# Attention and mixture of experts on one core: tokens sorted into lists per expert in DRAM for seven of eight groups

## The chip, the core and the metric

The kernel runs on one core of a Trainium2 chip. The core has five engines that work side by side, each with its own queue of instructions, which it executes in order: TensorE (PE) multiplies matrices, VectorE (DVE) and ScalarE (ACT) work element by element, GpSimd (POOL) does the same and issues some DMAs, and SyncE (SP) issues most of the others. Engines wait for one another through semaphores. SBUF is the on-chip memory of 128 partitions; PSUM holds matmul results. The metric is the device time of one execution in microseconds (us); the median of three runs counts. Less is better.

## The reference

The program is one transformer layer with the norms after the additions, on `x` of 2 sequences of 2048 tokens with 512 features, in float32. Attention has 16 query heads of 32 features that share one key and one value head, and is causal. The second half is a mixture of 8 experts, of which each token takes two.

```python
qkv = einsum('bsd,ed->bse', x, Wqkv_w) + Wqkv_b            # q: 512, k: 32, v: 32
scores = einsum('bqhd,bkd->bhqk', q, k) / sqrt(32)         # causal mask, softmax
ctx = einsum('bhqk,bkd->bqhd', softmax(scores), v)
x = layernorm(x + ctx @ out_w.T + out_b)
expert_scores = x @ router_w.T                             # 8 scores a token
top_scores, selected = top_k(expert_scores, 2)             # softmax of the two
h = silu(x_bf16[e's tokens] @ w1[e]) * (x_bf16[e's tokens] @ w3[e])    # 512 -> 128
routed = h @ w2[e]                                         # 128 -> 512
x = layernorm(x + sum over the two experts of top_scores * routed)
```

In the reference only the two chosen experts compute a token (`ragged_dot` over tokens sorted by expert).

## The kernel before

The 4096 tokens are 32 tiles T of 128 (16 for each sequence); four tiles are a group G. One function, `run`, holds all. It is called once with `full=False`, and a second time under `tc.If(flag)` only if a flag that the first pass computes says that its numbers cannot be trusted (softmax without an exact row maximum overflowed); in the runs here it isn't taken.

Work is written as Python generators that `yield step(engine, us, ...)` before they issue instructions. At build time the class `Order` (L67) simulates the engines with these assumed durations, with latencies between engines (`LAT`), buffers (`rings` of named tokens, and four PSUM `banks`), priorities and due times (`Due`), and so fixes one order of instructions for each of PE, ACT, DVE and POOL. The wrapper `InOrder` (L239) issues them, which is why nearly every line of the profile is L248. DMAs on SP are not held to that order: the framework's scheduler places them. On the chip each engine then follows its fixed list; where an assumed duration was wrong, the engine waits.

Per group, `project` (L519) loads four tiles `xg`, transposes them on PE, and computes keys, values and queries. Per tile, `attention` (L1067) goes through the tile's own key block and all earlier ones of the sequence, so that tile T has T modulo 16, plus one, **key steps**: 272 in all. A key step is: eight K=32 row-tiled score matmuls on PE into the PSUM tile `three` and one bank; two exponentials on ACT (`exponentials`, out to `acc` for the own block, to `pT` for the others); the product with the values on PE (`weigh`, tile `cs`); and an addition of `pT` into `acc` on DVE (`add_up`), which gives the row sums. The own block is masked by an `affine_select` on POOL before PE may use it. `pT` has three buffers. `three` has one, so PE writes the next scores only after ACT has read it.

At a tile's end `after` (L753) sums `acc` over keys on PE, forms the reciprocals on DVE, multiplies by the output weights on PE (`woT`), adds the residual `xr` (loaded by SP, bias added on POOL), and normalises (`layernorm`, L726: statistics on DVE, two tiny `r` operations on POOL, scaling on ACT).

`experts` (L841) then computes **all eight experts for every token** and multiplies by gates that are zero for six of them. For a tile: transposes and router (`route`, `gates`), 64 bf16 matmuls of 128x512 against w1 and w3 (`up`, `half`), tanh on ACT, a product with `a` on DVE, the gate on POOL (`a<-a,gt`), the product `h` on DVE, a DMA transpose `hT` on SP, 32 matmuls against w2 (`down`), the addition to `x` and a second layernorm. Groups 0 to 6 do this group by group, with due times some 16 tiles later, so that it fills gaps; the last group does it tile by tile. `x1` keeps up to four groups of 128x4x512 in SBUF until then. For the last tile, `last_sums` (L1187) adds the last two key blocks on PE instead of DVE; `judge` computes the flag's input before the last experts.

```python
def issue(self, ins):
    InOrder.last = ins
    return self.tc.keep_in_program_order(ins)
...
for c in range(NG):                                  # mm4: four column groups of 32
    mm(out[quad(c)], lhsT[:, quad(c)], rhs, **k)
```

Of the kernel before, what the change touches and what calls it, by code (L numbers as in the profile page):

```python
# [9 lines left out]
F32 = mybir.dt.float32  # L10
# [18 lines left out]
X1B = 4  # L29
# [37 lines left out]
class Order:  # L67
# [4 lines left out]
    LAT = {PE: 0.3, ACT: 0.15, DVE: 0.15, POOL: 0.15, SP: 0.0}  # L72
    LOOK = {DVE: 1.0}
    TURN = {FULL: 0.1, ROW: 0.2, COL: 0.115, TILE: 0.115}
    CAP = 5.0

    def __init__(self, banks, **rings):
        self.rings = {name: [n, []] for name, n in rings.items()}
        self.banks = [None] * banks
        self.busy = {e: 0.0 for e in self.LAT}  # L80
        self.sig = {}
        self.parked = []
        self.now = self.end = 0.0
        self.event = 0
        self.array = None
        self.count = 0
        self.dues = []
        self.held = {}
# [24 lines left out]
    def hold(self, ring, n):  # L113
        self.held[ring] = [self.take(ring) for _ in range(n)]
# [6 lines left out]
    def take_all(self, rings, t):  # L121
        slots = self.slots(rings.count(BANK), t)
        tokens = []
        for ring in rings:
            if ring == BANK:
                token = Token(ring)
                token.slot = slots.pop(0)
                token.before = self.banks[token.slot]
                self.banks[token.slot] = token
            else:  # L130
                token = self.take(ring)
            tokens.append(token)
        return tokens

    def slots(self, n, t):

        free = [i for i, k in enumerate(self.banks) if k is None or k.at is not None and k.at <= t + 1e-6]
        free.sort(key=lambda i: self.banks[i].at if self.banks[i] else 0.0)
        return free[:n]

    def room(self, rings):

        at = 0.0
        n = rings.count(BANK)
        if n:
            free = sorted(0.0 if k is None else k.at for k in self.banks if k is None or k.at is not None)
            if len(free) < n:
                return None
            at = free[n - 1]
        for i, ring in enumerate(rings):  # L150
            if ring == BANK:
                continue
# [30 lines left out]
    def run(self):  # L183
        while self.parked:
# [23 lines left out]
            if eng in self.LOOK and best[1][0].us > 1.0 and self.prio(best[1][0], urgent) > -0.9:  # L208

                for x in able:  # L210
                    s = x[1][0]
                    if (
                        s.eng == eng and self.prio(s, urgent) <= -0.9 and x[0] < t0 + self.LOOK[eng]
                        and x[0] <= best[0] + self.LOOK[eng]
                    ):
                        best = x
                        break
# [38 lines left out]
def mqa_postln_moe_postln(  # L256
# [22 lines left out]
    EB = 4  # L279
    scale = 1.0 / math.sqrt(HD)  # L280
# [15 lines left out]
    def mm4(out, lhsT, rhs, **k):  # L296
        for c in range(NG):
            mm(out[quad(c)], lhsT[:, quad(c)], rhs, **k)

    def tr4(out, in_):  # L300
        for c in range(NG):
            tr(out[quad(c), :], in_[:, quad(c)], ident)
# [14 lines left out]
    )  # L317
    warm = const.tile([P, 1], F32, name="warm")
# [4 lines left out]

    worst = const.tile([P, 1], F32, name="worst")
# [13 lines left out]

    def run(full):
# [5 lines left out]
        n_x1 = X1B - full  # L345
        x1p = es.enter_context(tc.tile_pool(name="x1p", bufs=n_x1))
        att = es.enter_context(tc.tile_pool(name="att", bufs=1))
        ptp = es.enter_context(tc.tile_pool(name="pt", bufs=3))
# [5 lines left out]
        if full:  # L354
# [19 lines left out]

        order = Order(
            NB, three=1, pT=3, acc=2, cs=1, c_sb=2, lT=1, ctxT=1, shT=3 if full else NSH, pmax=2, xg=1, xT=1,
            xr=2, qT=2, kv=GPB + 1, x1=n_x1, x1b=1, x1T=TG, a=2, h=2, hT=2,
# [46 lines left out]
        def load_weights():  # L424
            nat["wkv"] = ffn.tile([2 * HD, D], F32, tag="a", name="wkv_n")
            nat["wq"] = grp.tile([P, NHH, D], F32, tag="qT", name="wq_n", bufs=2)
            nat["wo"] = grp.tile([P, NHH, D], F32, tag="qT", name="wo_n", bufs=2)
            nat["wr"] = ffn.tile([E, D], F32, tag="a", name="wr_n")
            b_row = nat["b"] = ffn.tile([1, D + 2 * HD], F32, tag="x1T", name="b_row", bufs=TG)
# [7 lines left out]
        def turn_biases():  # L437
# [23 lines left out]
            free(order.held["x1T"][0])  # L461
# [45 lines left out]


        kT, v, qTs, kv_held, qT_held, st_x = {}, {}, {}, {}, {}, {}

        def load_x(G):
            b, gi = divmod(G, GPB)
            xg = grp.tile([P, TG, D], F32, tag="xg", name="xg")
            for t in range(TG):
                s0 = gi * GT + t * P
                nc.sync.dma_start(xg[:, t, :], x[b, s0 : s0 + P, :])
            return xg

        def project(G, due):  # L519
            hurry = -1.5 if G == 0 else None  # L520
            due = Due(due, 21.7)
            (hx,) = yield step(SP, 0.0, ["xg"])
            xg = load_x(G)
            st = {}

            def turn(t):
                (m,) = yield step(PE, 0.45, ["m"], array=FULL, lat=5.0 + 0.5 * t, prio=hurry, due=due)
                p_t = bank(m)
                for dc in range(NDC):
                    tr(p_t[:, dc * P : (dc + 1) * P], xg[:, t, dc * P : (dc + 1) * P], ident)  # L530
                if t == TG - 1:
                    free(hx)
# [214 lines left out]
        def add_keys(p_l, e, start, stop):  # L747
            for g in range(NG):
                mm(p_l[quad(g), :, :], ones, e[:, g, :, :], start=start, stop=stop)

        sums, contexts = {}, {}

        def after(T, acc, h):  # L753
# [3 lines left out]
            if T == seq[-1]:  # L757
                yield step(SP, 0.0, after=[("w", T, T % TPB - 2)])
            (h_xr,) = yield step(SP, 0.0, ["xr"])
            xr = grp.tile([P, D], F32, tag="xr", name="xr", bufs=2)  # L760
# [3 lines left out]
            if T == seq[-1]:  # L764
                yield step(SP, 0.0, after=[("l", T)])
            if T in sums:
                m, h_l, p_l = sums[T]
            else:
                m, h_l = yield step(PE, 0.87, ["m", "lT"], array=COL, due=due)
                p_l = bank(m, F32, (P, NHH, P))  # L770
                add_keys(p_l, acc, True, True)
# [4 lines left out]
            lT = att.tile([P, D // HD, HD], F32, tag="lT", name="lT")  # L776
# [8 lines left out]
            if T == seq[-1]:  # L785
                yield step(DVE, 0.7, after=[("c", T)])
            c_sb, h_c = contexts.pop(T)
            ctxT = att.tile([P, NHH, P], F32, tag="ctxT", name="ctxT")
# [5 lines left out]
            if T == seq[-1] and not full:  # L794
                spawn(judge())
# [12 lines left out]
            if t == 0:  # L808
                (x1_held[G],) = yield step(SP, 0.0, ["x1"])
                x1s[G] = x1p.tile([P, TG, D], F32, tag="x1", name="x1")  # L810
                mark("x1", G)
            yield step(DVE, 1.65, after=[("xr", T), ("x1", G)])
            y = x1s[G][:, t, :]
# [6 lines left out]
            if alone or t == TG - 1:  # L820
                spawn(
                    experts(G, [t] if alone else list(range(TG)), start_of((G + n_x1) * TG)),
# [3 lines left out]
        def judge():  # L826

            (h,) = yield step(DVE, 1.1, ["lT"])
            ok = att.tile([P, NT, D // HD], F32, tag="lT", name="ok")
            vec.tensor_scalar(ok, fine, LIMIT, None, ALU.is_le)  # L830
            vec.tensor_reduce(worst, ok, AX.XY, ALU.min)
            free(h)

        def residual(T, xr):
            yield step(POOL, 1.4, lat=3.0)
# [4 lines left out]

        def experts(G, ts, due):  # L841
            b, gi = divmod(G, GPB)
            x1 = x1s[G]
# [7 lines left out]
            x1b = ffn.tile([P, NDC, GT], BF16, tag="x1b", name="x1b", bufs=1)  # L851
# [3 lines left out]
            def route(t):  # L855
# [4 lines left out]
                for dc in range(NDC):  # L860
                    tr(p_t[:, dc * P : (dc + 1) * P], x1[:, t, dc * P : (dc + 1) * P], ident)
                yield step(ACT, 0.6)
                x1T = st["x1T", t] = ffn.tile([P, NDC, P], F32, tag="x1T", name="x1T", bufs=TG)
# [3 lines left out]
                if n > 1:  # L867
                    yield step(POOL, 1.05)
# [68 lines left out]
            def up(t, j):  # L937
# [8 lines left out]
                if j == 0:  # L946
                    st["h_h", t] = got[2]
                    st["h", t] = ffn.tile([P, E, FF], BF16, tag="h", name="h")
# [9 lines left out]
                a = ffn.tile([P, EB, FF], F32, tag="a", name="a")  # L958
# [6 lines left out]
                if n > 1:  # L965
                    yield step(POOL, 2.25)
# [33 lines left out]
            def down(t):  # L1000
# [4 lines left out]
                hT = ffn.tile([P, E, P], BF16, tag="hT", name="hT")  # L1005
# [21 lines left out]
                y = x1[:, t, :]  # L1027
# [3 lines left out]
                yield step(SP, 0.0)  # L1031
                s0 = gi * GT + t * P
                nc.sync.dma_start(out[b, s0 : s0 + P, :], y)
                if t == TG - 1:
                    free(x1_held[G])
# [31 lines left out]
        def attention():  # L1067
            for T in seq:
# [4 lines left out]
                for i, kt in enumerate([own] + list(range(own))):  # L1073
# [11 lines left out]
                    )  # L1085
                    qT = qTs[G]
# [26 lines left out]
        def exponentials(T, kt, parts, hp):  # L1113
# [18 lines left out]
            if kt == own:  # L1132

                yield step(POOL, 2.25, prio=-2.0)
# [10 lines left out]
        def weigh(T):  # L1145
# [5 lines left out]
            for i, kt in enumerate(kts):  # L1151
# [16 lines left out]
                if i == 0:  # L1168
                    spawn(add_up(T, [k for k in kts if k != own][: own - direct(T)]))
                    if direct(T):  # L1170
                        spawn(last_sums(T, kts[own + 1 - direct(T) :]))
                        spawn(after(T, None, None), True)
# [5 lines left out]
            c_sb = att.tile([P, D], F32, tag="c_sb", name="c_sb", bufs=2)  # L1178
            act.copy(c_sb, cs.rearrange("p h k -> p (h k)"))
            free(h_cs)  # L1180
            contexts[T] = c_sb, h_c
            mark("c", T)
            if not direct(T):
                yield step(SP, 0.0, after=[("sum", T)])
                spawn(after(T, *tiles.pop((T, own))))

        def last_sums(T, kts):  # L1187

            m, h_l = yield step(PE, 0.87, ["m", "lT"], array=COL, prio=-0.2, after=[("sum", T)])
            p_l = bank(m, F32, (P, NHH, P))  # L1190
            add_keys(p_l, tiles[T, T % TPB][0], True, False)
            for kt in kts:
                yield step(PE, 0.87, array=COL, prio=-0.2, after=[("p", T, kt)])
# [119 lines left out]
```

## Time and profile before

| what | value |
|---|---|
| runs | 1153.9, 1154.88, 1155.04 us; median 1154.88 |
| profiled execution | 1154.49 us, span on the core 1152.7 us |
| granted TensorE clock | 0.998 of full speed |
| attention's own key blocks start | T=0 at 40.5 us, T=10 at 271.9, T=16 (second sequence) at 562.9, T=26 at 812.6, T=31 at 1056.0 |
| last addition into `acc` ends | 1115.5 us |
| DMA | 40.94 MB, 36 GB/s over the span |
| two of PE's waits | PE `three` for ACT `pT` 21.4 us, PE `bank` for DVE `acc` 4.3 us |
| POOL's instructions `r` | shortest 543 ns, median 2487 ns (`r<-r,neg_half`, 128x1) |

The span runs from the first to the last instruction on the core; some 2 us of the execution's time lie around it. A group's mean is the time of one instruction from its start to its end; matmuls overlap one another, so the busy time of a group (the time in which at least one of them ran) is far less than count by mean. PE is busy for nearly the whole span, but it does four different things in turn, and the other engines' load rises with the number of key blocks of a tile: a late tile has fifteen additions on DVE, an early one none. So the span is best read in stages, cut where the tiles in the table start.

### The profile page before, as it was taken

How to read it: one execution, taken by the hardware profiler on the slowest of the kernel's cores; microseconds unless marked ns; L12 is line 12 of the kernel's file. 1: busy time of each engine (PE TensorE's matmuls, PEld its weight loads, DVE VectorE, ACT ScalarE, POOL GpSimd, SP SyncE). 2: the span in 40 equal slices, each digit the busy share in tenths (PEclk: the TensorE clock that was granted, in tenths of full speed). 3: DMA queues.
4: the chain of work that ended last, by engine and by line, in shares of the span. 5: the costliest groups of instructions: out<-in, count | busy, mean ns of one | idle time of the engine just before them, and what ended most of it. 6: DMA issues, size and time to landing. Idle time of an engine off the chain costs nothing.

```text
span 1152.7 us, 29615 instructions
## 1 busy us (share of the span) xinstructions
PE 1087.3 (94%) x13046; PEld 329.4 (29%) x13046; DVE 923.6 (80%) x1171; ACT 735.8 (64%) x839; POOL 452.2 (39%) x291
## 2 busy tenths in 40 slices
PE   8999999999999999999999999999999899899975
PEld 4322222222322233232222222223233233233222
DVE  2348767878998789989747877779989999999975
ACT  2455667576676677775656556666676667767561
POOL 3212432213451245445325324416556455345110
PEclk9999999999999999999999999999999999999999
DMA  9301001002110021111001000001011011011011
GB/s 253 75 17 56 10 10 48 11 11 56 30 47 1 11 66 29 38 30 38 19 20 56 20 10 19 20 20 38 20 37 40 20 26 42 19 30 48 20 29 31
DMA packets 57404, 40.94 MB, mean 36 GB/s; under 512 B 42729, under 2 KB 43753, under 8 KB 57266
## 3 DMA queue, kind: packets, MB, share of 16 engines
q1 hardware_dynamic: 47248, 34.63, 11.2%
q0 software_dynamic: 9360, 3.15, 2.4%
q8 instruction: 104, 1.70, 0.6%
q10 hardware_dynamic: 658, 1.18, 0.3%
q14 instruction: 34, 0.28, 0.1%
HBM read 25.58 MB, written 8.39 MB: 29 GB/s over the span
## 4 chain that ended last, share of the span: by engine, by line
PE 58%; DVE 28%; issue 5%; POOL 4%; ACT 4%; DMA 0%; DVEq 0%; ACTq 0%; POOLq 0%
PE bank L248 33%; DVE acc L248 15%; PE three L248 14%; PE cs L248 11%; ACT pT L248 2%; POOL r L248 2%; POOL a L248 2%; DVE st L248 2%; DVE x L248 2%; DVE h L248 2%; DVE lT L248 1%; DVE ctxT L248 1%; DVE a L248 1%; DVE fine L248 1%; DVE mx L248 1%
## 5 line engine op out<-in xcount | busy, mean ns | idle before, releaser
L248 DVE TENSOR_TENSOR acc<-acc,pT 128x2048 f32<-128x2048 f32 x238 | 559.1, 2349 | 36.7 <-PE cs L248 22.0
L248 ACT ACTIVATE pT<-three,bias 128x1536 f32<-128x1536 f32 x240 | 370.3, 1543 | 266.9 <-PE bank L248 211.2
L248 PE MATMUL three<-qT,kT_g 32*64 32x512 f32 x3264 | 299.5, 612 | 29.9 <-ACT pT L248 21.4
L248 PE MATMUL bank<-qT,kT_g 32*64 32x512 f32 (+1 forms) x1216 | 304.8, 590 | 0.2 <-ACT qT L248 0.2
L248 PE MATMUL cs<-pT,v_g 128*32 128x512 f32 x1920 | 255.4, 603 | 1.6 <-ACT c_sb L248 0.9
L248 POOL TENSOR_TENSOR r<-r,neg_half 128x1 f32<-128x1 f32 x64 | 100.6, 1572 | 360.1 <-DVE r L248 348.4
L248 POOL TENSOR_TENSOR a<-a,gt 128x512 f32<-128x512 f32 x56 | 115.1, 2060 | 164.2 <-DVE a L248 164.2
L248 ACT ACTIVATE pT<-bank,bias 128x512 f32<-128x512 f32 x240 | 163.6, 682 | 0.0
L248 PE MATMUL bank<-w_sb,x1b 128*32 128x512 bf16 x2048 | 127.3, 380 | 2.5 <-DVE x1b L248 0.7
L248 POOL TENSOR_SCALAR_AFFINE_SELECT acc<-acc 128x2048 f32<-128x2048 f32 x32 | 72.2, 2256 | 140.6 <-ACT acc L248 140.6
L248 PE MATMUL bank<-woT,ctxT 128*32 128x512 f32 x1024 | 119.7, 594 | 3.9 <-DVE ctxT L248 3.6
L248 PE MATMUL bank<-xT,wqT 128*32 128x512 f32 x1024 | 122.4, 594 | 0.0
L248 PEld LDWEIGHTS three<-qT,kT_g 32*64 32x64 f32 x3264 | 60.4, 129 | 194.7 <-ACT pT L248 138.5
L248 PEld LDWEIGHTS cs<-pT,v_g 128*32 128x32 f32 x1920 | 40.6, 108 | 178.0 <-issue 172.7
L248 POOL TENSOR_SCALAR r<-mv,r 128x1 f32<-128x1 f32 x62 | 83.7, 1350 | 6.1
L248 PEld LDWEIGHTS <-x1b 128*32 128x32 bf16 x2048 | 57.5, 97 | 84.4 <-issue 47.5
L248 ACT ACTIVATE acc<-three,bias 128x1536 f32<-128x1536 f32 x32 | 49.4, 1544 | 38.0 <-PE three L248 23.0
L248 PE MATMUL bank<-w_sb,hT 128*32 128x512 bf16 x1024 | 62.4, 379 | 2.5 <-DVE h L248 1.4
L248 ACT ACTIVATE x<-x,r 128x512 f32<-128x512 f32 x62 | 50.5, 818 | 6.5 <-POOL r L248 6.5
L248 PEld LDWEIGHTS bank<-woT,ctxT 128*32 128x32 f32 x1024 | 31.1, 109 | 79.9 <-issue 64.3
L248 DVE STREAM_TRANSPOSE lT<-bank 128x512 f32<-128x512 f32 x32 | 22.9, 715 | 38.4 <-PE bank L248 38.4
L248 DVE TENSOR_TENSOR x<-bank,xr 128x512 f32<-128x512 f32 x32 | 22.0, 688 | 39.1 <-PE bank L248 33.3
(110 smaller groups left out, 962.3 us busy)
## 6 DMA issues: line engine op xcount, KB each, us to landing
xg<-in_L_attn_x_dram SPq DMA_DIRECT2D x32, 256.0 KB, 4.0
xr<-in_L_attn_x_dram SPq DMA_DIRECT2D x32, 256.0 KB, 2.6
out_dram<-x SPq DMA_DIRECT2D x32, 256.0 KB, 2.0
w_sb<-in_L_ffn_w_dram POOLq DMA_DIRECT2D x8, 256.0 KB, 9.1
wq_n<-in_L_attn_Wqkv_w_dram ACTq DMA_DIRECT2D x4, 256.0 KB, 5.9
wo_n<-in_L_attn_out_w_dram SPq DMA_DIRECT2D x1, 1024.0 KB
w_sb<-in_L_ffn_w_dram POOLq DMA_DIRECT2D x1, 1024.0 KB, 15.7
hT<-h SPq DMA_TRANSPOSE x31, 3.1
```

The costliest lines, as they stand in the source:

```text
L248: return lambda *a, **k: self.issue(getattr(self.engine, name)(*a, **k))
```

## The change

For groups 0 to 6 the dense experts are replaced by lists of tokens in DRAM; group 7 keeps `experts`. The groups form four sets, (0,1), (2,3), (4,5) and (6,). Each has, for each expert, room for 448 tokens (256 in the last set), in a DRAM array `x_by` (bf16) of inputs and `y_by` (float32) of results.

- `clear` fills `x_by` with zeros: 16 DMAs on SP, 13 MB.
- `choose` does transposes and router as before, then computes each token's place in its two lists: a few small DVE operations, six small bf16 matmuls that count the tokens ahead of it, and `places`.
- `scatter` writes each tile to `x_by` twice by an indirect DMA on POOL, float32 in, bf16 out: 56 DMAs. The normalised tile is also written to `x1_d` in DRAM by SP (28 DMAs).
- `expert_set` loads each expert's list by a DMA transpose on SP (24 of 448 rows, 8 of 256), and `expert` multiplies it by w1 and w3, with the weights now as the stationary operand and the tokens as the moving one; tanh on ACT, two DVE products, no gate; `down` multiplies by w2 in parts of up to 128 tokens, copies the result on ACT, and writes it to `y_by` (112 DMAs on SP).
- `combine` and `second` read `x1_d` back (28 DMAs on SP), gather two rows of `y_by` for each token by indirect DMAs on POOL (56), add them with their shares on DVE, and normalise.
- The flag now also says whether a list overflowed; it is computed after `run`.
- `Order` gets other latencies, a look-ahead for PE, a `CAP` of 10 for due work instead of 5, longer assumed times for some steps and delays behind DMAs. `pT` has five buffers. Most 128x512 tiles are now `page`s from a pool of 20.
- For the last tile the PE sums of the last two blocks are no longer spread over the tile's end; they are one step of three after `cs` is done.

```diff
-X1B = 4
+PAGES = 20
+PT = 5
+X1 = 6
+SETS = (
+    ((0, 1), (448,), (58, 146)), ((2, 3), (448,), (172, 192)), ((4, 5), (448,), (210, 236)),
+    ((6,), (256,), (230, 259)),
+)
...
-    LAT = {PE: 0.3, ACT: 0.15, DVE: 0.15, POOL: 0.15, SP: 0.0}
-    LOOK = {DVE: 1.0}
+    LAT = {PE: 0.15, ACT: 0.08, DVE: 0.1, POOL: 0.5, SP: 0.0}
+    LOOK = {DVE: 1.0, PE: 0.25}
...
+        def clear(i_set, begin):
+            rows = x_by[i_set][:, :].rearrange("(p k) d -> p k d", p=P)
+            k = rows.shape[1] // 4
+            for i in range(4):
+                yield step(SP, 0.0, after=[("scores", begin + 3 * i)])
+                nc.sync.dma_start(
+                    rows[:, i * k : (i + 1) * k, :], zeros[:, None, :].to_broadcast([P, k, D])
+                )
...
-        def after(T, acc, h):
+        def after(T, terms, c_sb, h_c):
...
-            if T in sums:
-                m, h_l, p_l = sums[T]
-            else:
-                m, h_l = yield step(PE, 0.87, ["m", "lT"], array=COL, due=due)
+            m, h_l = yield step(PE, 0.87 * len(terms), ["m", "lT"], array=COL, due=due)
...
-            if alone or t == TG - 1:
+            if G in set_of and not full:
+                if t == TG - 1:
+                    spawn(choose(G))
+                yield step(SP, 0.0, lat=2.5)
+                nc.sync.dma_start(x1_d[T * P : (T + 1) * P, :], y)
+            elif alone or t == TG - 1:
...
+        def choose(G):
...
+            mm(
+                p_n[:, : TG + 1, :], ones_b, both[:, TG, None, :].to_broadcast([P, TG + 1, E]),
+                start=True, stop=False,
+            )
+            for t in range(TG):
+                mm(
+                    p_n[:, t + 1 :, :], ones_b,
+                    both[:, t, None, :].to_broadcast([P, TG - t, E]), start=False, stop=False,
+                )
+            mm(flat[:, : TG * E], tri, both[:, :TG, :].rearrange("p t e -> p (t e)"), start=False, stop=True)
...
+        def scatter(T):
+            i_set = set_of[T // TG]
+            for k in range(2):
+                yield step(POOL, 1.45, after=[("clear", i_set)])
+                ins = gps.indirect_dma_start(
+                    out=x_by[i_set][:, :], out_offset=place(T, k), in_=x1s[T], in_offset=None,
+                    bounds_check=E * room[i_set] - 1, oob_is_err=False,
+                )
...
+            yield step(SP, 0.0, lat=4.5)
+            free(x1_held[T])
+            mark("there", T)
...
+        def expert_set(i_set, between):
...
+                    now = begin_ + (end - begin_) * (e * len(parts) + i) // (E * len(parts))
+                    (h_x,) = yield step(
+                        SP, 0.0, ["x1b"], after=[("there", T) for T in Ts] + [("scores", now)]
+                    )
+                    xT = ffn.tile([P, NDC, n], BF16, tag="x1b", name="xbT", bufs=2)
+                    got = nc.sync.dma_start_transpose(xT, x_by[i_set][at_ : at_ + n, :])
...
+        def expert(i_set, e, at_, n, xT, h_x, due):
...
+            for dc in range(NDC):
+                mm4(p1, w1_sb[:, dc, e, :], xT[:, dc, :], start=(dc == 0), stop=(dc == NDC - 1))
+            spawn(other())
+            yield step(ACT, 0.2 + 0.4 * n / GT)
+            a = page(h_a, (n,))
+            act.activation(a, p1, AF.Tanh, scale=0.5)
+            yield step(DVE, 0.1 + 0.6 * n / GT)
+            vec.scalar_tensor_tensor(a, a, 1.0, p1, ALU.add, ALU.mult)
...
+            vec.tensor_mul(h, st["p3"], a)
...
+        def down(i_set, e, at_, h, due, h_h):
+            m, h_y = yield step(PE, 0.25, ["m", "y"], due=due)
...
+            mm4(p_y, h, w2_sb[:, e, :], start=True, stop=True)
...
+            act.copy(y[:rows, :], p_y)
+            free(m)
+            yield step(SP, 0.0)
+            nc.sync.dma_start(y_by[i_set][at_ : at_ + rows, :], y[:rows, :])
...
+        def combine(i_set, Ts):
...
+                nc.sync.dma_start(y, x1_d[T * P : (T + 1) * P, :])
...
+                    yield step(POOL, 1.4)
+                    part = page(h_g[k])
+                    gps.indirect_dma_start(
+                        out=part, out_offset=None, in_=y_by[i_set][:, :], in_offset=place(T, k),
+                        bounds_check=E * room[i_set] - 1, oob_is_err=False,
+                    )
...
+        def second(T, y, h_x, parts, h_g):
...
+            for k in range(2):
+                yield step(DVE, 0.7 + 0.95 * k)
+                vec.scalar_tensor_tensor(y, parts[k], shares[:, k, T : T + 1], y, ALU.mult, ALU.add)
+                free(h_g[k])
+            yield from layernorm(y)
+            yield step(SP, 0.0, lat=2.5)
+            nc.sync.dma_start(out[b, i * P : (i + 1) * P, :], y)
```

The pair of numbers in `SETS`, such as (58, 146), says between which of the 272 key steps the set's eight experts are spread.

## The prediction

> **What bounds the kernel now.** I read busy shares first, then the span cut into stages, then single rows. The page's first part and the chain of work that ended last:
>
> ```profile
> PE 1087.3 (94%) x13046; PEld 329.4 (29%) x13046; DVE 923.6 (80%) x1171; ACT 735.8 (64%) x839; POOL 452.2 (39%) x291
> PE 58%; DVE 28%; issue 5%; POOL 4%; ACT 4%; DMA 0%; DVEq 0%; ACTq 0%; POOLq 0%
> ```
>
> PE looks like the bound, but over a quarter of the chain is DVE. So I cut the span where tiles T=0, 10, 16, 26 begin and where the last addition runs (columns: stretch, length, busy time and instructions of each engine, granted clock, DMA share, GB/s):
>
> ```profile
> 0.00:40.00 40.00, 34.17 (x270) 15.65 (x270) 11.48 (x34) 7.83 (x12) 9.11 (x17) 1.00 1.07 208
> 40.00:272.00 232.00, 228.34 (x2466) 62.62 (x2462) 161.15 (x185) 151.10 (x174) 68.16 (x43) 1.00 0.10 31
> 272.00:563.00 291.00, 278.02 (x3570) 82.81 (x3566) 264.58 (x290) 206.48 (x228) 127.11 (x78) 1.00 0.13 32
> 563.00:813.00 250.00, 245.20 (x2798) 71.40 (x2790) 185.66 (x235) 155.06 (x180) 102.67 (x64) 1.00 0.09 25
> 813.00:1114.00 301.00, 278.25 (x3676) 86.67 (x3668) 278.09 (x358) 207.24 (x234) 143.27 (x85) 1.00 0.12 30
> 1114.00:1153.00 39.00, 23.32 (x291) 10.26 (x291) 22.61 (x75) 8.07 (x15) 1.91 (x4) 0.93 0.10 30
> ```
>
> Stages 40-272 and 563-813 are PE's (98%), with DVE at 69 and 74%. Stage 813-1114 has both at 92%. The same stretches for the expert weights alone (PE busy):
>
> ```profile
> 40.00:272.00 232.00, 5.05 (x80) 1.00 0.10 31
> 272.00:563.00 291.00, 65.54 (x1072) 1.00 0.13 32
> 563.00:813.00 250.00, 24.03 (x384) 1.00 0.09 25
> 813.00:1114.00 301.00, 82.19 (x1344) 1.00 0.12 30
> ```
>
> The experts sit almost wholly in the two stages where DVE is nearly as full as PE. This decides the case: what the change takes from PE there is worth only what DVE lets through.
>
> **Removed and added on PE.** The chain in order of time shows 32 expert matmuls start to start:
>
> ```profile
> 847.75 1.73 PE bank L248 x32
> ```
>
> That is 54 ns each. Dense: 28 tiles x 96 x 54 ns = 145 us. Lists of 448: for each expert 32 matmuls at 448/512 of 54 ns, 1.51 us, and w2 in four parts of four column groups (the 64-row part uses two, and lasts as long), 16 x 54 = 0.86 us; 2.38 x 8 experts x 3 sets = 57 us. The list of 256: 32 x 27 + 8 x 54 ns = 1.3 us x 8 = 10 us (no bf16 matmul of 256 columns is in the trace; if it cost as much as 512, 17). The 42 counting matmuls at the 59 ns of `neg_ident,mx` (7.6 us / 128): 2.5 us. Net: 145 - 70 = **75 us less PE**. Router and its transposes stay.
>
> I compared both orders of instructions, cut at the same key steps. Expert matmuls by stage before: 80, 1072, 384, 1536 (the last with the tail). After: none; 294; 260; and 1254, of which 368 have 448 columns and 256 have 256, while 384 are group 7's dense ones. Priced as above: 4, 58, 21, 83 us against 0, 14, 13, 58. Projections move a little: 64 matmuls from the first to the second stage, 48 from the third to the fourth (3.5 and 2.6 us), 12 of `woT` like the first (0.7). So PE changes by -8, -39, -10, -22 us.
>
> **DVE.** Rows:
>
> ```profile
> L248 DVE TENSOR_TENSOR acc<-acc,pT 128x2048 f32<-128x2048 f32 x238 | 559.1, 2349 | 36.7 <-PE cs L248 22.0
> L248 POOL TENSOR_TENSOR r<-r,neg_half 128x1 f32<-128x1 f32 x64 | 100.6, 1572 | 360.1 <-DVE r L248 348.4
> L248 POOL DMA_DIRECT2D w_sb<-in_L_ffn_w_dram x9 | 8.1, 931 | 0.3 <-POOL w_sb L248 0.3
> ```
>
> A dense tile costs DVE four products of 0.68 us, an addition of 0.68 and statistics of 1.03 (695 + 182 + 154 ns). A list of 448 costs two products of 0.60, and `second` two of 0.68 and the same statistics for each tile. Overall little changes (some 10 us less), but it moves. Stage 272-563: before 43 products, 12 additions, 12 statistics = 50 us; after 14 products of 448 columns = 8.5; **-41**. Stage 563-813: 17.7 before; after 12 x 0.60 + 16 x 0.68 + 8 x 1.03 = 26, and 2 us of place arithmetic; **+10**. Stage 813-1114: 65 before (52 products, 16 quarter ones of 0.345, 14 additions, 14 statistics); after 22 x 0.60 + 16 x 0.41 + 4 x 0.68 + 16 x 0.345 + 37 x 0.68 + 2 x 0.68 + 20 x 1.03 = 75; **+10**: combining sets 1 to 3 falls where DVE has fifteen additions a tile.
>
> **ACT** gains 112 copies of `y` parts at the 0.58 us of its other copies (65) and has 32 tanh of 0.35 to 0.53 us for 56 of 0.60 (-18): +47 us, to 783 of some 1110; no bound by itself.
>
> **The score loop.** With one `three`, scores wait for the exponential. In the timeline near the end, where nothing else was in the way:
>
> ```profile
> 1107.50 1.54 ACT L248 ACTIVATE pT<-three,bias 128x1536 f32<-128x1536 f32 x1 [1.63 <-PE bank L248]
> 1110.29 1.54 ACT L248 ACTIVATE pT<-three,bias 128x1536 f32<-128x1536 f32 x1 [0.67 <-PE bank L248]
> ```
>
> 2.78 us a key step, which the change keeps: 81 steps in either late stage are 225 us.
>
> **Stage by stage.** 0-272: PE's, -8; the 13 MB of `clear` are placed among the first loads by the new order. At the 253 GB/s of the page's first slice they take 52 us of DMA; the loads of group 2 queued between them are needed only near 80 us, so I take +3 (0 to +15 if SP, in order, holds up `xr` and `xg`). 272-563: PE 278 - 39 = 239, DVE 265 - 41 = 224, loop 225. At PE's own 95.5% this is 250; with three bounds within 7% I take 254: **-37**. 563-813: PE 235 at 98%: **-10**. 813-1114: DVE 278 + 10 = 288. The additions' mean, 2349 ns, lies over their median of 2286 ns; POOL's `a<-a,gt` goes, so I give 4 back: 284 at 92.4% is 307, at 95% 299; I take 304: **+3**, while PE falls to 256 and idles. Tail: 39 + 5: the three sums in one step (2 x 0.87 beyond the last and a wait for the copy of `cs`, about 2.6 us) and the flag after `run` (two wide operations of 0.42 and 0.69 us and some small ones, 2.3 us). Sum: -8 + 3 - 37 - 10 + 3 + 5 = **-44 us**, from the profiled 1154.49 (0.4 under the median): **1110 us**.
>
> **Queues and waits.** SP goes from 130 DMAs to 305; at 0.33 us an issue (`xr` row; 1.24 for a transpose of 256 KB, some 2.2 for 448 rows) about 150 us, no bound. But a `y_by` store waits on ACT and a list's load on all scatters, and behind either in SP's queue stand `xr` loads. `xr` lands in 2.6 us and is needed only after the sums, reciprocals and `woT`, some 8 us; that hides it, and past 8 us each late microsecond is PE's. Traffic roughly triples from 41 MB (a third of the DMAs' time at 253 GB/s).
>
> POOL loses `a<-a,gt` (115 us) and the casts (33), and gains 112 indirect DMAs. The nearest row is `w_sb`, 931 ns an issue: 104 us, POOL 408 us. The Trainium skill speaks against that: *SBUF — State Buffer*, section "SBUF: two separate sides", says GpSimd cannot write its descriptors while VectorE holds their shared port, and gets it when that operation ends. The `w_sb` issues ran at 12-20 us, with DVE nearly idle. The trace shows the lock on another row: `r` takes 543 ns alone and 2487 in the median, most of an addition of 2.35 us more. By the rule an issue is up to 0.93 + 2.35 = 3.3 us, 370 in all, POOL 674 us. The page ties it to perf modes, or two SBUF inputs against a reading GpSimd operation; whether an indirect DMA counts no row shows. An addition runs half the time and leaves half its length on average, so I take 0.93 + 0.6 = 1.5 us, near the 1.4 to 1.45 that the order assumes. Queued behind eight scatters are the `affine_select` of a later tile and the `r` of layernorms; PE's `cs` waits for the former.
>
> **Rivals.**
> - *All of PE's saving arrives*: DVE runs at 98% in the last stage too and holds nobody up. 1154 - 74 = 1080. For: the longer look-ahead, five `pT`. Against: DVE's 92% in the last stage, and +10.
> - *POOL's queue, slower*: every issue costs 3.3 us, 1.85 over what the order assumes, x 112 = 207 us of lateness, in bursts of eight (15 us) before an `affine_select`. If a third of it reaches PE or DVE, 70 us, the time is 1180. It decides from 44/112 = 0.4 us an issue that gaps don't absorb. For: `r`'s median. Against: bursts come at group ends, POOL is 39% busy.
> - *SP's queue*: late `xr` and list loads, 1 us for each of 32 tiles: 1140.
> - *It doesn't do what it says*: an overflowing list sets the flag and the second pass runs, over 2000 us. The reference's router puts at most 394 tokens (of 448) and 196 (of 256) on an expert: 1%.
>
> **How the numbers follow.** Forecast 1110 (own range 1090 to 1135): 0.50. PE's saving in full, 1080: 0.20. SP's queue, 1140: 0.10. No change: 0.02. POOL, slower, 1180: 0.17. Second pass 0.01. So faster 0.80, within 0.2% (some 2.3 us, about what a measurement can tell) 0.02, slower 0.18. From 1068 (the full saving and a third of PE's 38 us of idle mid-span) to 1165, which leaves out the worse half of the POOL case.
>
> **What would show it.** Right: PE near 1010 us, DVE near 910; stage T=10 to 16 near 254 us with the rest nearly unchanged, T=26 to the last addition over 290 us with DVE above 92% and PE below 87%. Wrong: last stage under 285 us (the DVE bound), POOL issues over 2.5 us with PE `cs` waiting for POOL (the queue), PE waiting for `xr` or lists (SP).

## The result and the profile after

The changed kernel takes **1191.35 us** (median of 4 runs, 1189.26 to 1195.32) against 1154.45 before: 1.032 times the time, 95% interval 1.030 to 1.035. The forecast was 1110, and the range ended at 1165. The profiled execution took 1195.32 us, with a span of 1193.5.

First the page of the changed kernel, busy times and granted clock:

```profile
PE 1047.9 (88%) x11824; PEld 298.0 (25%) x11824; DVE 912.3 (76%) x1202; ACT 778.0 (65%) x927; POOL 474.6 (40%) x322
PEclk9999999999999989999899999999899999899976
```

DVE and ACT are near the forecast's 910 and 783. PE is 38 us over its 1010, but at a mean granted clock of 0.959: the same matmuls take 1026.1 us in a run further down (`both_off_pool`, clock 0.987). So the work is nearly as light as it was said to be, and yet no engine is busy for 90% of the time. The stages, cut at the same tiles as before (stretch, length, busy time and instructions of each engine, clock, DMA share, GB/s):

```profile
0.00:43.00 43.00, 36.28 (x273) 16.18 (x274) 12.22 (x43) 8.05 (x13) 10.07 (x20) 1.00 1.15 283
43.00:266.00 223.00, 210.03 (x2263) 56.09 (x2262) 157.71 (x183) 146.90 (x165) 77.22 (x43) 0.98 0.30 82
266.00:532.00 266.00, 252.59 (x2925) 64.48 (x2919) 229.33 (x226) 203.27 (x226) 84.90 (x42) 0.99 0.24 57
532.00:791.00 259.00, 237.30 (x2649) 69.34 (x2645) 197.53 (x302) 169.80 (x209) 132.06 (x92) 0.98 0.37 100
791.00:1141.00 350.00, 280.80 (x3450) 79.71 (x3447) 289.70 (x364) 240.06 (x299) 164.42 (x116) 0.94 0.52 140
1141.00:1194.00 53.00, 30.86 (x291) 12.23 (x285) 25.84 (x88) 9.93 (x18) 5.95 (x11) 0.75 0.12 38
```

Lengths before were 40, 232, 291, 250, 301 and 39 us. The second and third stages gained 9 and 25; the fourth lost 9, the fifth 49, the tail 14. In the fifth neither DVE (83%) nor PE (80%) is full: somebody waits. The list of waits names who (engine and tile, for whom, us in total, times, the longest):

```profile
ACT page L278 <- POOL r L278: 45.0, 12, 8.2
PE cs L278 <- POOL acc L278: 31.9, 4, 14.5
POOL x_by L278 <- DVE places L278: 16.3, 4, 14.3
```

Before, these waits were (PEld is PE's loading of weights):

```profile
ACT x L248 <- POOL r L248: 6.5, 7, 2.4
PEld cs L248 <- POOL acc L248: 2.0, 3, 0.8
```

How one such wait comes about is seen in the timeline, POOL's rows at tile T=7 and then the PE row that waited (start, us, engine, instruction, and in brackets the idle time before it and its releaser):

```profile
145.35 1.28 POOL L278 TENSOR_TENSOR page<-page,bo_sb 128x512 f32<-128x512 f32 x1
160.92 2.89 POOL L278 DMA_INDIRECT x_by<-page,places  x1 [14.28 <-DVE places L278]
164.11 2.28 POOL L278 DMA_INDIRECT x_by<-page,places  x1 [0.30 <-issue]
...
176.23 0.98 POOL L278 DMA_INDIRECT x_by<-page,places  x1 [0.30 <-issue]
177.21 1.29 POOL L278 TENSOR_TENSOR page<-page,bo_sb 128x512 f32<-128x512 f32 x1
178.43 2.04 POOL L278 TENSOR_SCALAR_AFFINE_SELECT acc<-acc 128x2048 f32<-128x2048 f32 x1
...
180.52 1.94 PE L278 MATMUL cs<-acc,v_g 128*32 128x512 f32 x8 [8.34 <-POOL acc L278]
```

POOL stands still from 146.6 to 160.9 at the head of its queue, for `places`. Then eight scatters run until 177.2, and a bias addition. Behind them stands the `affine_select` of T=7's own key block, which ACT had finished at 160.5. PE has nothing left from 172.2 and idles for 8.3 us. The wait for `places` itself cost next to nothing here, since they were there at 160.6, as soon as `acc`; what cost was to run eight scatters first. The longest wait, at T=30, has no wait for `places` in it at all:

```profile
998.74 0.68 ACT L278 ACTIVATE acc<-bank,bias 128x512 f32<-128x512 f32 x1
...
1000.60 1.00 POOL L278 DMA_INDIRECT x_by<-page,places  x1 [0.30 <-issue]
...
1017.08 1.00 POOL L278 DMA_INDIRECT page<-y_by,places  x1 [0.30 <-issue]
1018.08 2.04 POOL L278 TENSOR_SCALAR_AFFINE_SELECT acc<-acc 128x2048 f32<-128x2048 f32 x1
1020.17 1.94 PE L278 MATMUL cs<-acc,v_g 128*32 128x512 f32 x8 [14.49 <-POOL acc L278]
```

`acc` is ready at 999.4, and POOL then starts five scatters and six gathers (and a bias addition) before it masks it.

At this point the theory was the forecast's rival: scatters that last longer than planned (1.77 us and a gap of 0.30, for 1.45) hold up POOL's queue. Its rivals: late transfers on SP, DVE as the bound, or the new plan itself.

### The profile page after: what moved, and what is told of

It is laid out like the page before. It is cut to its first block, busy times and chain, and to the rows that moved or that the text cites. A ratio compares the mean times of both kernels' runs of the same rounds, so it can differ in the third digit from the quotient of the medians.

```text
span 1193.5 us, 27946 instructions
## 1 busy us (share of the span) xinstructions
PE 1047.9 (88%) x11824; PEld 298.0 (25%) x11824; DVE 912.3 (76%) x1202; ACT 778.0 (65%) x927; POOL 474.6 (40%) x322
## 5 line engine op out<-in xcount | busy, mean ns | idle before, releaser
L278 PE MATMUL bank<-woT,page 128*32 128x512 f32 x1024 | 126.8, 612 | 7.9 <-DVE page L278 6.9
L278 PE MATMUL bank<-xT,wqT 128*32 128x512 f32 x1024 | 128.5, 602 | 0.0
L278 POOL DMA_INDIRECT page<-y_by,places x56 | 78.8, 1407 | 103.6 <-DVE r L278 34.8
L278 POOL DMA_INDIRECT x_by<-page,places x56 | 98.8, 1765 | 46.4 <-issue 16.6
L278 ACT COPY page<-bank 128x512 f32<-128x512 f32 (+2 forms) x145 | 79.2, 597 | 38.8 <-PE bank L278 29.7
L278 DVE TENSOR_TENSOR page<-bank,page 128x512 f32<-128x512 f32 x36 | 24.8, 689 | 75.4 <-PE bank L278 58.7
L278 ACT ACTIVATE page<-page,r 128x512 f32<-128x512 f32 x62 | 50.3, 817 | 45.0 <-POOL r L278 45.0
L278 PE MATMUL cs<-acc,v_g 128*32 128x512 f32 x256 | 38.5, 672 | 31.9 <-POOL acc L278 31.9
L278 POOL TENSOR_SCALAR r<-mv,r 128x1 f32<-128x1 f32 x62 | 63.7, 1028 | 6.1
L278 POOL TENSOR_TENSOR page<-page,bo_sb 128x512 f32<-128x512 f32 x32 | 59.8, 1869 | 0.1
L278 PE MATMUL bank<-xbT,w_sb 128*32 128x448 bf16 (+1 forms) x1024 | 54.9, 341 | 2.4 <-DVE page L278 1.6
```

Of the source, the lines that this page charges most:

```text
L278: return lambda *a, **k: self.issue(getattr(self.engine, name)(*a, **k))
```

## The experiments

### The indirect DMAs off POOL

`scatter_off_pool`, at the same place in the plan, with the gathers left alone:

```diff
-                ins = gps.indirect_dma_start(
-                    out=x_by[i_set][:, :], out_offset=place(T, k), in_=x1s[T], in_offset=None,
-                    bounds_check=E * room[i_set] - 1, oob_is_err=False,
-                )
+                at_ = 2 * P * (T - SETS[i_set][0][0] * TG) + P * k
+                ins = nc.sync.dma_start(x_by[i_set][at_ : at_ + P, :], zeros)
```

> The 56 indirect writes into the lists are taken off POOL: at the same place SP writes a tile of zeros to fixed rows instead. The sort and so the lists' contents are left out; the order of every other instruction is the same. POOL's queue as the cause: POOL's 98.8 us of scatter issues and their wait for the places go, PE cs for POOL acc falls from 31.9 to under 5 us, the granted clock rises from 0.96 to 0.98 or more, and the time falls to 1125-1155 us. SP or DMA lateness: SP has 56 more DMAs and as many bytes, so 1190 us or more. DVE as the bound of the last stage: DVE's work is the same, so within 1% of 1191. The new plan (delays, look-ahead, due times) as the cause: the order is the same, so within 1% of 1191.

`both_off_pool` replaces the gathers in the same way:

> As the run before it, and the 56 gathers too: SP reads fixed rows instead. Left out are the sort and the choice of rows. POOL's queue as the cause: all 178 us of indirect issues leave POOL, ACT page for POOL r falls from 45 us to under 20, the PE gaps from 130 us to 60 or less, clock 0.99, and the time is 1090-1125 us, near the 1110 of the forecast. SP or DMA lateness: 1190 or more. DVE as the bound, or the plan: no further fall after the run before, both near 1191; if only the scatters matter, this run is within 10 us of it.

| kernel | us, median | ratio to before, 95% |
|---|---|---|
| scatter_off_pool | 1153.5 | 0.999 (0.998 to 1.001) |
| both_off_pool | 1122.9 | 0.973 (0.971 to 0.974) |

The indirect DMAs on POOL cost 68 us: 38 go with the scatters, another 31 with the gathers. SP takes 112 DMAs more and the kernel gets faster, so SP is out. DVE has the same work (920 us), so it did not set the loss. PE's idle time (span less busy time) falls from 146 to 93 us, less far than expected, and ACT's wait for `r` from 45 to 14.8. Both runs also leave out the sort, and their transfers go to fixed rows.

`fixed_rows_on_pool` leaves the scatters on POOL, as plain DMAs (`gps.dma_start(..., zeros)`) that need no places:

> The scatters stay on POOL, but write a tile of zeros to fixed rows by plain DMAs that wait for no places. The sort is left out. If the length of an issue is the cause (a lock with DVE's additions): an issue still takes 1.7-1.8 us in the mean and the time stays at 1175-1195. If the wait of POOL's queue for late places is the cause: issues may be as long, but they start when the order reaches them, PE cs for POOL acc falls under 10 us and the time to 1135-1165. Rivals without POOL: within 1% of 1191.

1153.5 us, as fast as without them on POOL. That looks like the wait for `places`; but the row of the scatters had changed too (shortest, median and longest issue in ns):

```profile
L278 POOL DMA_DIRECT2D x_by<-zeros x56: 539/539/671, 163.7 to 980.1; - x56
```

An issue of a plain DMA takes 0.54 us instead of a median of 2.0, so length and wait were changed together, and the run does not tell them apart. As the next part shows, a third thing changed with them: a plain DMA keeps its place in POOL's order.

### Spreading the scatters, and a miss that led on

`spread` (the computation is whole) holds each scatter in the plan until a later key step:

```diff
-                spawn(scatter(Ts[t]))
+                spawn(scatter(Ts[t], order.event + 2 + 2 * t))
...
-        def scatter(T):
+        def scatter(T, begin):
...
-                yield step(POOL, 1.45, after=[("clear", i_set)])
+                yield step(POOL, 1.45, after=[("clear", i_set), ("scores", begin + k)])
```

> The computation is whole. Each of a group's eight scatters is held until a later key step, one a key step from two key steps after the places' step was planned, so that the bursts of eight go and the places have two key steps (some 5 us) of slack. POOL's queue: no burst, PE cs for POOL acc falls from 31.9 to under 10 us, PE gaps from 130 to 90-105 us, time 1145-1170 us. DVE or the plan as the cause: within 1% of 1191. Against: a tile of x1 is held longer (six are there), which could cost PE up to some us a group.

**1216.3 us**, 1.054 of before (1.052 to 1.056): slower than the changed kernel, which no theory had said. ACT's wait for `r` is 65.9 us (45.0), PE's for `acc` 38.3 (31.9), and PE waits once for a list, 15.2 us; why these grew was not settled. In its trace the scatters of the first group still ran before T=7's `affine_select`, although the plan held them back. So the plan's order was laid beside the order of the built program. In the plan of the *unmodified* changed kernel POOL does `affine_select` of T=7 first, then four scatters, `r`, four scatters and a bias addition. In the built program, as in the trace above, all eight scatters come first, with the bias addition. At T=30, two of the five scatters and all six gathers that POOL started before the ready `acc` stand behind the `affine_select` in the plan.

The reason is in the wrapper. `keep_in_program_order` ties an instruction behind the one traced just before it on its engine. An indirect DMA with a bounds check, as written here, brings a register move with it, which does not pass through the wrapper. POOL as traced:

```
AffineSelect  I-1481
RegisterMove  I-1494     tied to nothing
DMACopy       I-1495     tied to I-1494 only
RegisterMove  I-1514     tied to nothing
DMACopy       I-1515     tied to I-1514 only
```

So at each of 112 places the chain is cut, and the framework's scheduler is free to put the DMA earlier, and with it what is tied behind it. Register moves are not shown in a profile. With plain DMAs for scatters (`fixed_rows_on_pool`) there are 56 such moves fewer, and the scatters stay where the plan has them; the gathers still float.

### POOL's order held

`pool_order_held` ties each instruction also to those that the wrapper issued before it on its engine (to all since the last that is no DMA, because the `declare_no_dep` between two scatters lifts a tie between them too):

```diff
...
     def issue(self, ins):
         InOrder.last = ins
+        here = {i.name for i in self.tc.nc.cur_bb.bb.instructions}
+        for i in self.behind:
+            if i.name in here:
+                self.tc.add_manual_dep(
+                    ins.ins, i.name,
+                    mybir.DependencyInfo(mybir.DependencyClass.NoSync, mybir.DependencyReason.DATA),
+                    reason="behind those before",
+                )
+        self.behind = (self.behind if "DMA" in type(ins.ins).__name__ else []) + [ins.ins]
         return self.tc.keep_in_program_order(ins)
```

> The computation is whole; the plan and every other engine's order are those of the changed kernel. An indirect DMA brings a register move of its own, and the wrapper ties an instruction only to the one traced just before it on its engine, so each of the 112 indirect DMAs is tied to its own move and to nothing earlier: in the built program they stand ahead of affine_select, r and bias additions that the plan puts first. Here each instruction on an engine is also tied to the ones issued before it, and POOL follows the plan. Theory (POOL's order, not the length of an issue): PE cs for POOL acc falls from 31.9 to under 8 us, the longest PE gap in mid-span under 5 us, clock 0.98 or more, time 1115-1140 us. Rival (an issue is too long beside DVE's additions, in whatever order): the gaps are smaller but remain, 1160-1185 us. Rival (SP, DVE or the plan): 1180 or more.

**1145.4 us** (1143.9 to 1146.8), 0.992 of before (0.991 to 0.994): 46 us less than the changed kernel, with the same instructions. In the two built programs PE, ACT and DVE have the same order, on SP one pair of neighbours is swapped, and POOL now follows the plan throughout; so the 46 us are POOL's order. That lies 5 us above the span of the one theory and 15 under that of the other; PE's wait for `acc` is 9.1 us (forecast under 8), its longest gap in mid-span 3.9, the clock 0.977 (forecast 0.98 or more):

```profile
PE cs L278 <- POOL acc L278: 9.1, 4, 2.9
ACT page L278 <- POOL r L278: 24.6, 12, 4.2
```

The same place in its timeline:

```profile
160.11 4.10 POOL L278 TENSOR_SCALAR_AFFINE_SELECT acc<-acc 128x2048 f32<-128x2048 f32 x1 [13.96 <-ACT acc L278]
164.39 1.13 POOL L278 DMA_INDIRECT x_by<-page,places  x1 [0.18 <-DVE den L278]
...
169.33 2.30 POOL L278 DMA_INDIRECT x_by<-page,places  x1 [0.30 <-issue]
171.62 1.92 POOL L278 TENSOR_TENSOR r<-r,neg_half 128x1 f32<-128x1 f32 x1
...
179.54 0.98 POOL L278 DMA_INDIRECT x_by<-page,places  x1 [0.30 <-issue]
180.51 1.33 POOL L278 TENSOR_TENSOR page<-page,bo_sb 128x512 f32<-128x512 f32 x1
...
171.63 1.06 PE L278 MATMUL cs<-acc,v_g 128*32 128x512 f32 x8
```

POOL masks `acc` first, and PE's `cs<-acc` starts 8.9 us earlier (0.5 of these from an earlier start of the tile), with no idle time before it.

What is left is split by `held_scatter_off`: order held, and the scatters off POOL.

> POOL's order held, and the scatters taken off POOL as in scatter_off_pool (the sort is left out). What is left between pool_order_held (1145.4) and both_off_pool (1122.9) is 22.5 us. If the length of the scatters still costs (103 us of issues, 1.84 in the mean for 1.45 in the plan): 1128-1136. If in the right order scatters are hidden and the rest is the gathers': 1141-1146.

1125.4 us, a little below the span of the first case. So 46.0 us were the order, 20.0 the scatters where they stand in the right order, and the gathers, once in order, cost 2.4, near the spread of the runs. (With no indirect DMA on POOL, the built order is the same with and without the new ties, so `both_off_pool` may stand beside the others here.) The gathers' 31 us of the first two runs were nearly all order too: with the scatters off POOL, holding the order alone brings 28.1 (1153.5 to 1125.4).

### What the length costs, and how it can be hidden

`held_and_true_times` tells the plan the measured sizes (2.0 and 1.7 us):

> As the run before it, and the plan is told 2.0 us for a scatter and 1.7 for a gather (the trace: 1.77 + 0.30 and 1.41 + 0.30) where it had 1.45 and 1.4. If what is left of POOL's waits comes from the sizes in the plan, this is 5-15 us faster than the run before; if the order alone was the cause, within 4 us of it.

1158.4 us: 13 slower instead of 5 to 15 faster. The new plan also moves other work; PE now waits 7.3 us for a list. True sizes alone are no remedy, and here a plan that differs a little differs by this much on the chip.

`held_late_sums_gathers_spaced` and `held_and_spread` build on the run with late sums on PE (next part). The first lets a tile's gathers go a key step or two after the last tile's; the second also holds the scatters as `spread` did, one key step earlier.

> The computation is whole: POOL's order held, late sums on PE, and a tile's two gathers are let go only a key step (two in the first two sets) after those of the tile before, so that no six gathers stand in a row. If bursts of gathers cost what is left: 5-12 us below the 1138.1 of the run without the spacing. If their number and length do, wherever they stand, no gain: 1136-1145.

> The computation is whole: POOL's order held, late sums on PE, gathers spaced as in the run before, and a group's eight scatters let go one a key step, as in spread, but now in an order that POOL keeps. In spread the key steps could not hold the scatters back, since they floated; so its 1216 says nothing of bursts. If eight scatters in a row, each 0.7 us longer than planned (1.84 + 0.30 for 1.45), are what costs the 20 us between pool_order_held and held_scatter_off: 1118-1130. If each scatter costs wherever it stands, or tiles of x1 held longer cost as much: 1131-1142.

1135.4 us (1134.3 to 1139.2) against 1138.1 (1136.2 to 1140.4) without the spacing: hardly beyond the runs' spread, so bursts of gathers were not what cost (its second case, missed by half a microsecond). And **1126.7 us** for the spread scatters, 0.977 of before (0.975 to 0.980), 8.7 below the run without, as the burst theory had it. That bursts were the cause is not shown: PE's wait for `acc` falls only from 2.4 us to none and ACT's for `r` stays (11.3 and 12.5), while the stage from T=16 to T=26 gets 11 us shorter (251.8 to 241.0). The new plan moved other work too, which alone made 13 us in `held_and_true_times`. This is the fastest kernel here that does the whole computation. Its page:

```profile
PE 1031.2 (92%) x11904; PEld 298.6 (27%) x11904; DVE 895.6 (80%) x1192; ACT 776.3 (69%) x927; POOL 497.8 (44%) x322
PEclk9999999999999999999999999999999999999996
```

POOL is busier than in the changed kernel (497.8 us for 474.6), and yet PE no longer waits for its `acc`, and ACT waits 12.5 us for `r` where it waited 45: the load was not the trouble.

### Is DVE the bound of the last stage? Is the plan at fault?

> POOL's order held, and for the last six tiles the last two key blocks are added up on PE, as the last tile does already: 10 additions (5 tiles) fewer on DVE, 23 us, and some 9 us more on PE, in the stage from T=26. If DVE bounds that stage (the forecast's step), it gets 8-20 us shorter; if POOL or the score loop does, no change or some us longer, as pT is held longer.

```diff
         def direct(T):
-            return 2 if T == seq[-1] else 0
+            return 2 if T >= NT - 6 else 0
```

1138.1 us, 7.3 less than with the order alone, for a DVE relieved of 30 us in all. The stage from T=26 to the last addition, of which the expectation spoke, got only 2.5 us shorter, with 25 us less of DVE's work in it (`pool_order_held`, then this run; columns as above, DVE's busy time third):

```profile
762.90:1096.00 333.10, 280.07 (x3468) 81.00 (x3460) 293.09 (x364) 241.58 (x302) 177.44 (x116) 0.96 0.55 148
761.20:1091.80 330.60, 288.95 (x3584) 85.44 (x3580) 267.64 (x369) 243.72 (x305) 172.42 (x121) 0.97 0.55 151
```

The other 5 came behind the last addition (47.6 to 42.5 us). That speaks against DVE as the bound. With the indirect DMAs off POOL:

> Scatters and gathers off POOL as in both_off_pool (sort and choice of rows left out), and the last two key blocks of the last six tiles added on PE. If DVE bounds the last stage once POOL is out of the way (in both_off_pool the tiles T=28, 30 and 31 have DVE at 96 to 98%): the stage falls from 321 to 300-310 us and the time to 1100-1112, more than the 7 us that the same step brought with the gathers on POOL. If DVE is no bound: 1116-1123.

1114.6 us, 8.4 less, between the two cases. The stage itself, from T=26 to the last addition, did not get shorter (752.5 to 1075.3 us, 323 against 321): T=28 fell from 50.5 to 43.9 us, T=29 rose from 52.4 to 57.9, and the gain, 8 us, again came behind the last addition. Tile by tile in `both_off_pool` (T=28, T=30 and the last tile; columns as above, DVE third):

```profile
843.00:893.00 50.00, 41.59 (x540) 11.25 (x532) 48.82 (x45) 40.27 (x51) 18.58 (x10) 1.00 0.49 124
...
945.60:1013.90 68.30, 55.77 (x786) 19.09 (x782) 65.24 (x117) 48.42 (x64) 21.93 (x20) 0.98 0.56 155
1013.90:1074.00 60.10, 46.30 (x582) 12.74 (x575) 58.04 (x60) 42.47 (x49) 24.74 (x11) 0.99 0.36 106
```

DVE is at 96 to 98% in these three, at 80 and 81% in T=26 and T=29: it may bind in these, but 23 to 25 us less of its work did not shorten the stage. What sets the stage was not settled.

For the plan itself:

> The changed kernel's plan (delays, look-ahead, CAP, longer times, pages, last sums in one step) with dense experts for all eight groups and no lists; pT has three buffers, since 16 tiles of x1 must be kept. If the plan itself cost the 37 us: 1185 or more. If the lists' DMAs on POOL did: 1140-1165, within 1% of before.

1168.7 us, 1.013 of before (1.011 to 1.014), between the two cases: so the plan is not free by itself, but this kernel has three `pT` where the changed one has five (and more pages and tiles of `x1`), and these were not told apart. It also has the ties of `pool_order_held`.

## Why the prediction was wrong

- **The step that failed** is the one on queues: "Queued behind eight scatters are the `affine_select` of a later tile and the `r` of layernorms; PE's `cs` waits for the former." It was written as a risk, and priced by the *length* of an issue (1.5 us, "near the 1.4 to 1.45 that the order assumes"), with "bursts come at group ends, POOL is 39% busy" against it. Both take for granted that POOL's order is the plan's. It isn't: scatters and gathers float ahead of the `affine_select` and `r` that the plan put first, and these then stand behind up to eight indirect DMAs that the plan puts after them (at T=7 and T=30). That cost 46 us by `pool_order_held`, more than the 37 by which the kernel got slower. The whole way from 1110 to 1191 is 46.0 us for the order, 20.0 for scatters on POOL in the right order, 2.4 for gathers, and 13 that remain without any indirect DMA on POOL (1122.9). The two orders of instructions had been compared for what they do to PE; POOL's, read against the plan, would have shown it before any run.
- **The term that was mis-sized** is the issue: 1.77 us in the mean for a scatter, 1.41 for a gather. Over both that is 1.59, near the 1.5; but the 0.30 us between two had no term, so each takes 1.9 in all. The rival's 3.3 was far too much. That scatters still cost 20 us in the right order fits this; how much of it is length was not measured by itself.
- **The POOL rival** (1180) had the right place and side. Its mechanism, 1.85 us of excess on each issue, was not it: the excess over the plan was some 0.5 us. That its number came near 1191 is luck in part.
- **SP's queue** did not bind: with 112 DMAs more on SP the kernel got faster.
- **The sums without POOL** were right for most of the span. The forecast's stages end at 267, 521, 761, 1065 and 1109 us; `both_off_pool` has 256, 514, 752, 1074 and 1119. Of the first 11 us, some 4.5 come from the 64 projection matmuls that move: they were priced at the 54 ns of a bf16 matmul, and float32 ones take 125 (128.5 us / 1024). T=0 starts 0.6 to 2.5 us later than before in the kernels with lists, within the 3 us given to `clear`.
- **The last stage** was forecast at 304 us and takes 321 even then. DVE's work there is 293, not 284: the mean addition got longer (2422 ns, from 2349) where 4 us had been given back for a shorter one. The rest is its 91% instead of 92.4. But that DVE's share sets this stage, as the forecast had it, is not shown: with 24 us less of DVE's work it stayed as long (323). This step stays open.
- **The tail** was forecast at 44 us; it is 45 in `both_off_pool` and 52 in the changed kernel, at clocks of 0.77 and 0.75.

## What to carry to other kernels

When an order is written out by hand, compare it with the built program on every engine, and most of all where instructions are of a new kind: helpers that an operation brings along (a register move here) can cut the chain that holds the order. A queue's share of busy time says nothing of this: POOL went from 40% busy in the changed kernel to 44 in the fastest one. Ask of each instruction what stands behind it in its queue, and put those that nobody needs soon behind those that others wait for.

## What the hardware showed beside

**Short idle times of PE cost twice.** The changed kernel around its longest gap (PE idle from 1005.7 to 1020.2 us; columns as above, the clock third from the end):

```profile
1006.00:1008.00 2.00, 0.00 (x0) 0.00 (x0) 1.35 (x10) 0.94 (x2) 1.39 (x3) 1.00 0.42 66
1008.00:1012.00 4.00, 0.00 (x0) 0.00 (x0) 0.00 (x0) 0.00 (x0) 3.08 (x4) 0.79 0.62 117
1012.00:1016.00 4.00, 0.00 (x0) 0.00 (x0) 0.00 (x0) 0.00 (x0) 3.52 (x4) 0.50 0.90 158
...
1022.00:1024.00 2.00, 2.00 (x23) 0.35 (x20) 1.75 (x1) 0.00 (x0) 0.00 (x0) 0.50 0.00 0
1024.00:1028.00 4.00, 3.55 (x48) 0.79 (x40) 4.00 (x12) 2.52 (x3) 1.02 (x1) 1.00 0.10 12
```

If the clock fell from full to half at once, the mean of 0.79 places that at some 1010.3, and it is back at 1024.0. So it halves some 4.6 us into the gap and comes back some 3.8 us after PE resumed. In between eight `cs` matmuls take 1.94 us instead of 1.06. The same 11824 matmuls keep PE busy for 1047.9 us here, and less with the order held (`pool_order_held`, clock 0.977) and with POOL free of the indirect DMAs (`both_off_pool`, 0.987):

```profile
PE 1036.8 (91%) x11824; PEld 296.4 (26%) x11824; DVE 918.2 (80%) x1202; ACT 777.3 (68%) x927; POOL 490.1 (43%) x322
PE 1026.1 (92%) x11824; PEld 295.5 (26%) x11824; DVE 920.0 (82%) x1202; ACT 777.9 (70%) x927; POOL 324.4 (29%) x210
```

So some 22 us of PE's busy time go with the clock. The Trainium skill, *TensorE: Matmul & The Clock Gate*, section on the HAM clock gate, gives about 3.4 us for either way, near what these windows show; the 0.4 to 1.2 us more lie within what windows of 2 and 4 us can tell.

**An indirect scatter's issue is longer beside DVE's additions; a plain DMA's is not.** In the changed kernel the 56 scatters take 0.98 us at the shortest, 2.0 in the median and 3.0 at the longest. The 20 of them that met no addition into `acc` took 0.98 to 1.06 us, the 36 that met one up to 3.04, 2.25 in the median. The plain DMA in `fixed_rows_on_pool`, at the same steps of the plan, takes 0.54 us in the median and 0.67 at the longest, and 41 of those 56 met an addition. So something like the prediction's lock is there for these indirect DMAs, at 0.8 us in the mean (1.77 - 0.98) where 2.35 was feared. Which of their properties brings it is not shown: the plain DMA also casts nothing and reads half the bytes.
